# Transposing the attention output on VectorE, and the output product for two tiles at once

## The chip, the cores and the metric

The kernel runs on one core of a Trainium2 chip. The metric is the device time of one execution in microseconds. The program is a single launch; three runs of the kernel before are given, and one more execution was taken with the hardware profiler.

## What is computed

The input is `x` of shape (4, 512, 128): four batches of 512 tokens with 128 features. One causal attention layer with 16 heads of 64 comes first, and then six layers, each with a windowed attention and a feed-forward part. Layer `i`, cut to what matters here:

```python
def local_attention(q, k, v):        # windows of 32 tokens
    bk2, bv2 = look(bk), look(bv)    # keys and values: the window before and the window itself
    sim = einsum('bhwie,bhwje->bhwij', bq, bk2) * 8.0
    attn = softmax(where(mask, -max, sim), -1)
    return einsum('bhwij,bhwje->bhwie', attn, bv2)

def attn_layer(x, Wqkv, qs, ksc, Wo):
    q, k, v = split(x @ Wqkv)        # 16 heads of 64
    q, k = l2norm(q) * qs, l2norm(k) * ksc
    q = q * cos * scale + rotate_half(q) * sin * scale
    k = k * cos * inv + rotate_half(k) * sin * inv
    return local_attention(q, k, v) @ Wo

for i in range(6):
    x = attn_layer(shift_tokens(x), ...) + x
    x = ffn_layer(shift_tokens(x), ...) + x    # layernorm, W1, gelu gate, W2
```

All of it is in float32; the mask is a bfloat16 table.

## The kernel before

**Stages.** The first attention runs for about 560 us and is not touched, apart from its hand-over. Then come the layers. A unit (`class Unit`, line 530) is one tile of 128 tokens of one batch of one layer: 6 layers, 4 batches and 4 tiles `T` give 96 units. `slot(n, ...)` (line 893) is one step of a software pipeline: it makes the scores and the attention of unit `n` (`u`), the output product of unit `n-1` (`prev`), the transposed q and k of unit `n+1` (`nxt`), and the projections of unit `n+2` (`new`). The order of the instructions on each engine is the order in which this function writes them (`tc.manual_schedule`, line 983); the framework adds the waits between engines. Feed-forward steps of an earlier batch are planned into slots (lines 998 to 1008): over four slots these are a token shift and a chunk (T = 0), the mean and a chunk (T = 1), the variance and the second product `out` (T = 2), the scale and a chunk (T = 3). They are `Ffn` (line 757) with `layernorm_steps` (line 92).

**One unit, in the order of the work.** `project` (line 535) makes 128x1024 of q, k or v in a PSUM tile of two banks. `square` (549) is on ACT, `sum_squares` (553) on DVE. `rotate` (558) makes two products on DVE from the same PSUM tile, lines 561 and 567; `add_rotated` (577) adds them on POOL. `inverse_norms` (580) bounds the sums of squares from below on DVE and takes the inverse root: a shift and a subtraction on integers on DVE (84, 85), and three Newton rounds of four small operations on POOL (87 to 90). `over_norm` (585) multiplies on POOL. `transpose_q` and `transpose_k` (654, 659) go through PE and an ACT copy.

`scores` (670) writes the mask with eight matmuls on tiles of 64 rows by 32 columns of the PE array, adds 64 score products, then on DVE takes the maximum `mx` (697) and subtracts it (699). `exponents` (703) is one ACT instruction over 128x1024. `transpose_p` (707) transposes through PE and copies with ACT. `times_v` (712) is PV: window `j` on the rows of the output, the value windows in `u.vw`; two DVE operations per half divide by the denominator (728, 729) into `on`.

`v_windows` (628) copies v to `vt` on ACT, writes that to DRAM and reads it back as overlapping windows with four more DMAs, all on SP's queue. `transpose_o` (736) transposes `on` with eight PE transposes and two ACT copies into `aT`. `project_out_2` (741) is the output product of one tile with eight matmuls of 128 columns, and `residual` (746) adds x on DVE.

**PSUM.** `two_t` (516) hands out three tiles of two banks in rotation, so that scores, PV's first half and v share tile 0 of a slot, q, PV's second half and feed-forward tile 1, and k has tile 2, which is tile 0 of the next slot. `one_t` (520) is a ring of two single banks for transposes and small products.

**Tables of ACT.** Exponentials and Gelu need different tables. After the Gelu of a slot, line 981 runs an exponential on two columns (`prime`), so that the table is there for the next slot.

**Order of a slot before.** PE: scores, q, a feed-forward norm step, output product of `prev`, first half of k and the transposes of p between, second half of k, PV, `qT`, v, `kT`, feed-forward, transposes of `on`. ACT: square of q, exponents, copies of `pT`, square of k, copies of `qT`, `vt`, `kT`, Gelu, copies of `aT`. DVE: `mx`, subtraction, norm step, rotation of q with the residual between, PV's division, sum of q, rotation of k, sum of k, bound, gate.

Of the kernel before, what the change touches and what calls it, by code (L numbers as in the profile page):

```python
# [15 lines left out]
P = 128  # L16
# [16 lines left out]
def body(ctx: ExitStack, tc: tile.TileContext, a, out: bass.AP):  # L33
# [16 lines left out]
    dram = ctx.enter_context(tc.tile_pool(name="dram", bufs=1, space=bass.MemoryType.DRAM))  # L50
# [10 lines left out]
    hsel = const.tile([P, 2], F32, tag="hsel", name="hsel")  # L61
    nc.vector.memset(hsel, 0.0)
    nc.vector.memset(hsel[0:HD, 0:1], 1.0)
    nc.vector.memset(hsel[HD:P, 1:2], 1.0)
# [10 lines left out]
    prime = small.tile([P, 2], F32, tag="prime", name="prime", bufs=1)  # L75


    def rsqrt(v, n, eng):
# [7 lines left out]
        for k in range(3):  # L86
            eng.tensor_tensor(t, y, y, ALU.mult)  # L87
            eng.tensor_tensor(t, t, v, ALU.mult)
            eng.tensor_scalar(t, t, -0.5, 1.5, ALU.mult, ALU.add)
            eng.tensor_tensor(y if k < 2 else v, y, t, ALU.mult)  # L90

    def layernorm_steps(state, bank, inT, outT, g=None, b=None, eng=nc.vector, nt=NT, temp=tmpt, later=None):
# [16 lines left out]
        def var():  # L109
# [5 lines left out]
            then(lambda: rsqrt(rs, nt, eng))  # L115

        def scale():
# [7 lines left out]
            if g is not None:  # L125
                then(lambda: nc.vector.tensor_scalar(h, h, g, b, ALU.mult, ALU.add))
# [363 lines left out]
    s2a = ps2a = s2b = s2 = ps_one = kT_first = vts = vds = None  # L490
# [88 lines left out]

    def inverse_norms(u):  # L580

        nc.vector.tensor_scalar(u.ss, u.ss, 1e-24, None, ALU.max)  # L582
        rsqrt(u.ss, 2 * HEADS, nc.gpsimd)
# [16 lines left out]
    def second_step():  # L600

        nonlocal s2b, ps_one, kT_first, vts, vds
# [5 lines left out]
        vts = [s2b.tile([P, 2, NC, HD + 1], F32, tag=f"vt{j}", name=f"vt{j}") for j in range(2)]  # L608
        for t_ in vts:
            nc.gpsimd.memset(t_[:, :, :, HD : HD + 1], 1.0)  # L610
        vds = [dram.tile([W + S, 2, NC * (HD + 1)], F32, tag=f"vd{j}", name=f"vd{j}") for j in range(2)]
        for d_ in vds:
            nc.sync.dma_start(out=d_[0:W], in_=a["zeros"])
# [14 lines left out]
    def v_windows(u):  # L628


        vt, vd = vts[u.n % 2], vds[u.n // NT % 2]
        src = u.p[2].rearrange("p (c a d) -> p a c d", a=2, d=HD)
        for c in range(2):
            nc.scalar.copy(vt[:, c, :, 0:HD], src[:, c])  # L634
        r0 = u.T * P
        nc.sync.dma_start(out=vd[r0 + W : r0 + W + P], in_=vt.rearrange("p a c d -> p a (c d)"))
        u.vw = s2b.tile([P, NW, NC, HD + 1], F32, tag="vw", name="vw", bufs=2)
        for odd in range(2):
            rows = vd[r0 + odd * W : r0 + odd * W + P].rearrange("(j k) a x -> a k j x", k=2 * W)
            for c in range(2):  # L640
                nc.sync.dma_start(
                    out=u.vw[c * HD : (c + 1) * HD, odd::2].rearrange("p j c d -> p j (c d)"), in_=rows[c]
                )
# [25 lines left out]

    def scores(u):  # L670

        sc = two_t(0, "ps_att")
        for j in range(NW):
            for h in range(2):
                rows = slice(h * HD, (h + 1) * HD)
                mm(  # L676
                    sc[j * W : (j + 1) * W, h, :],
                    lhsT=ident16[rows, h * HD : h * HD + W],
                    rhs=band[rows, min(u.T + j, 1)].unsqueeze(1).to_broadcast([HD, NC, 2 * W]),
                    start=True,  # L680
                    stop=False,
                    skip_group_check=True,
                )
        for c in range(NC):
            for j in range(NW):
                for h in range(2):
                    mm(  # L687
                        sc[j * W : (j + 1) * W, h, c * 2 * W : (c + 1) * 2 * W],
                        lhsT=u.qT[h * HD : (h + 1) * HD, c, j * W : (j + 1) * W],
                        rhs=u.kT[h * HD : (h + 1) * HD, c, j * W : (j + 2) * W],  # L690
                        start=False,
                        stop=True,
                        skip_group_check=True,
                    )
        s3 = sc.rearrange("p a (c n) -> p a c n", n=2 * W)
        mx = small.tile([P, 2, NC], F32, tag="mx", name="mx")
        nc.vector.tensor_reduce(mx, s3, AX.X, ALU.max)
        u.pr = s2.tile([P, NC, 2, 2 * W], F32, tag="pr", name="pr", bufs=2)
        nc.vector.tensor_tensor(
            u.pr.rearrange("p c a n -> p a c n"), s3, mx.unsqueeze(3).to_broadcast([P, 2, NC, 2 * W]), ALU.subtract  # L700
        )

    def exponents(u):
        u.prf = u.pr.rearrange("p c a n -> p (c a n)")
        nc.scalar.activation(u.prf, u.prf, AF.Exp)

    def transpose_p(u, g):
        if g == 0:
            u.pT = s2.tile([P, NC, P], F32, tag="pT", name="pT", bufs=2)
        transposed(u.prf, g, u.pT, 0)  # L710

    def times_v(u, g):
        if g == 0:
            u.on = s2.tile([P, NC, 2, HD], F32, tag="on", name="on", bufs=1)
        o = two_t(g, "ps_att")
        for c in range(4):
            for j in range(NW):
                for h in range(2):
                    mm(  # L719
                        o[j * W : (j + 1) * W, h, c * (HD + 1) : (c + 1) * (HD + 1)],  # L720
                        lhsT=u.pT[h * HD : (h + 1) * HD, 4 * g + c, j * W : (j + 1) * W],
# [451 lines left out]
```

## Time and profile before

| | us |
|---|---|
| median of three runs | 2180.27 (2177.94 to 2182.57) |
| profiled execution | 2177.22 |
| its span | 2175.2 |
| PE busy (matmul) | 2127.0 |
| PE weight loads | 1424.5 |
| DVE busy | 1720.1 |
| ACT busy | 1380.8 |
| POOL busy | 1508.3 |
| first slot's scores, from the start | 561.0 |
| last slot's scores, from the start | 2134.3 |

The busy times count instructions at work on an engine within the span; matmuls are pipelined, so PE's busy time tells that something was in the array, not how well it was filled. The time of an execution is 2.0 us longer than the span of its profile. Most lines below are of three kinds: groups (line of code, engine, operation, output from inputs, shape, count, busy us, mean ns, idle time before and what ended it), timelines (start us, length us, engine, line, operation, count, and in brackets the idle time before), and stages (length, then busy us of PE, PE's weight loads, DVE, ACT and POOL, the granted clock, DMA share and GB/s).

### The profile page before, as it was taken

How to read it: one execution, taken by the hardware profiler on the slowest of the kernel's cores; microseconds unless marked ns; L12 is line 12 of the kernel's file. 1: busy time of each engine (PE TensorE's matmuls, PEld its weight loads, DVE VectorE, ACT ScalarE, POOL GpSimd, SP SyncE). 2: the span in 40 equal slices, each digit the busy share in tenths (PEclk: the TensorE clock that was granted, in tenths of full speed). 3: DMA queues.
4: the chain of work that ended last, by engine and by line, in shares of the span. 5: the costliest groups of instructions: out<-in, count | busy, mean ns of one | idle time of the engine just before them, and what ended most of it. 6: DMA issues, size and time to landing. Idle time of an engine off the chain costs nothing.

```text
span 2175.2 us, 80486 instructions
## 1 busy us (share of the span) xinstructions
PE 2127.0 (98%) x35150; PEld 1424.5 (65%) x35150; DVE 1720.1 (79%) x2501; ACT 1380.8 (63%) x2677; POOL 1508.3 (69%) x2279
## 2 busy tenths in 40 slices
PE   7999999999999999999999999999999999999998
PEld 5655656555566666676667666666766676667665
DVE  3776766767778888888888888888888888888884
ACT  3675656755455667666676666676666666666764
POOL 2554545455787787777877877877877778778773
PEclk8999999999999999999999999999999999999999
DMA  3000000000343353343434334433453344434331
GB/s 126 1 1 1 1 1 1 1 1 1 100 111 99 99 135 101 101 114 99 120 111 109 102 100 128 116 91 111 106 136 92 101 119 112 115 103 114 91 101 41
DMA packets 88812, 180.17 MB, mean 83 GB/s; under 512 B 9327, under 2 KB 23405, under 8 KB 88429
## 3 DMA queue, kind: packets, MB, share of 16 engines
q1 hardware_dynamic: 87756, 173.31, 29.3%
q8 instruction: 278, 4.55, 0.9%
q10 hardware_dynamic: 704, 1.70, 0.2%
q14 instruction: 74, 0.60, 0.1%
HBM read 122.81 MB, written 52.43 MB: 81 GB/s over the span
## 4 chain that ended last, share of the span: by engine, by line
PE 87%; DVE 9%; POOL 1%; ACT 1%; issue 1%; DMA 0%; SPq 0%; DVEq 0%; POOLq 0%; ACTq 0%
PE ps_proj L539 21%; PE ps_one L649 15%; PE ps_one L744 7%; PE ps_att L719 6%; PE ps_sc L299 6%; PE ps_att L687 5%; PE ps_o L384 5%; PE ps_pt L364 5%; PE ps_proj L808 3%; PE ps_proj L788 2%; PE ps_proj L789 2%; PE ps_pj L278 1%; PE ps_att L676 1%; DVE ss L556 1%; PE ps_pj L268 1%; DVE ss L582 1%
## 5 line engine op out<-in xcount | busy, mean ns | idle before, releaser
L578 POOL TENSOR_TENSOR rot<-rot,t 128x1024 f32<-128x1024 f32 x192 | 454.3, 2367 | 176.2 <-DVE t L567 161.4
L539 PE MATMUL ps_proj<-wqkv,xs 128*128 128x512 f32 x1152 | 569.6, 602 | 0.2
L353 POOL TENSOR_TENSOR pr<-pr,den 128x1024 f32<-128x1024 f32 x128 | 240.9, 1892 | 248.9 <-DVE den L350 239.0
L586 POOL TENSOR_TENSOR rot<-rot,ss 128x1024 f32<-128x1024 f32 x192 | 361.8, 1905 | 7.4
L551 ACT ACTIVATE sq<-ps_proj 128x1024 f32<-128x1024 f32 x192 | 196.5, 1024 | 172.4 <-PE ps_proj L539 145.0
L539 PEld LDWEIGHTS ps_proj<-wqkv,xs 128*128 128x128 f32 x1152 | 188.5, 190 | 102.9 <-issue 93.8
L561 DVE TENSOR_TENSOR rot<-ps_proj,lt 128x1024 f32<-128x1024 f32 x192 | 233.8, 1217 | 6.0 <-ACT sq L551 5.2
L567 DVE TENSOR_TENSOR t<-ps_proj,lt 128x1024 f32<-128x1024 f32 x192 | 233.2, 1215 | 0.0
L556 DVE TENSOR_REDUCE ss<-sq 128x16 f32<-128x1024 f32 x192 | 232.3, 1210 | 0.0
L339 ACT ACTIVATE pr<-ps_sc,nm 128x128 f32<-128x128 f32 (+3 forms) x448 | 220.3, 509 | 11.8 <-DVE nm L326 8.6
L649 PEld LDWEIGHTS ps_one<-ident,rot 128*128 128x128 f32 x1536 | 171.6, 141 | 66.9 <-issue 43.3
L649 PE MATMUL ps_one<-ident,rot 128*128 128x128 f32 x1536 | 204.6, 276 | 5.2 <-POOL rot L586 4.5
L326 DVE TENSOR_REDUCE nm<-ps_sc 128x2 f32<-128x1024 f32 x128 | 156.0, 1219 | 64.6 <-PE ps_sc L314 64.5
L744 PEld LDWEIGHTS ps_one<-aT,wo 128*128 128x128 f32 x1536 | 182.9, 192 | 23.7 <-issue 23.0
L652 ACT COPY pT<-ps_one 128x512 f32<-128x512 f32 x192 | 110.1, 586 | 136.5 <-PE ps_one L649 136.4
L744 PE MATMUL ps_one<-aT,wo 128*128 128x128 f32 x1536 | 189.2, 276 | 0.4 <-DVE rs L114 0.3
L719 PEld LDWEIGHTS ps_att<-vw,pT 64*32 64x32 f32 x12288 | 130.9, 105 | 77.0 <-ACT pT L652 69.0
L728 DVE RECIPROCAL rden<-ps_att 128x8 f32<-128x8 f32 x192 | 39.0, 203 | 174.0 <-PE ps_att L719 173.9
L634 ACT COPY vt<-ps_proj 128x512 f32<-128x512 f32 x192 | 103.2, 590 | 97.2 <-PE ps_proj L539 90.9
L652 ACT COPY qT<-ps_one 128x512 f32<-128x512 f32 x192 | 103.1, 589 | 96.0 <-PE ps_one L649 96.0
L87 POOL TENSOR_TENSOR yt<-y 128x32 f32<-128x32 f32 (+2 forms) x384 | 87.7, 228 | 108.0 <-DVE y L85 62.0
L364 PEld LDWEIGHTS ps_pt<-ident,pr 128*128 128x128 f32 x1024 | 117.2, 141 | 58.5 <-issue 47.7
(171 smaller groups left out, 4164.2 us busy)
## 6 DMA issues: line engine op xcount, KB each, us to landing
vw<-vd SPq DMA_DIRECT2D x384, 260.0 KB, 4.9
vd<-vt SPq DMA_DIRECT2D x96, 520.0 KB, 2.7
wqkv<-in_wqkv_dram SPq DMA_DIRECT2D x18, 512.0 KB, 4.9
wo<-in_wo_dram SPq DMA_DIRECT2D x6, 512.0 KB, 7.2
w<-in_w_dram SPq DMA_DIRECT2D x6, 341.0 KB, 6.3
xr<-in_x_dram SPq DMA_DIRECT2D x3, 256.0 KB, 7.4
scales<-in_scales_dram SPq DMA_DIRECT2D x6, 128.0 KB, 4.5
w<-in_w_dram SPq DMA_DIRECT2D x12, 64.0 KB, 5.5
```

The costliest lines, as they stand in the source:

```text
L339: nc.scalar.activation(self.pr[:, h, cols], self.sc[:, h, cols], AF.Exp, bias=self.nm[:, part_, h : h + 1], accum_out=self.den[:, part_, h ...
L353: nc.gpsimd.tensor_tensor(self.pr, self.pr, self.den[:, 0].unsqueeze(2).to_broadcast([P, 2, S]), ALU.mult)
L364: nc.tensor.transpose(pt[:, k * P : (k + 1) * P], self.pr[:, h, k * P : (k + 1) * P], ident)
L539: mm(p[:, c, :], lhsT=u.xs[:, u.T * P : (u.T + 1) * P], rhs=wpart[j][:, c * 512 : (c + 1) * 512], start=True, stop=True,)
L556: nc.vector.tensor_reduce(u.ss[:, j * HEADS : (j + 1) * HEADS], heads(u.sq[j]), AX.X, ALU.add)
L561: nc.vector.tensor_tensor(heads(t0), heads(pf), lt[:, u.T, 2 * j].unsqueeze(1).to_broadcast([P, HEADS, HD]), ALU.mult)
L567: nc.vector.tensor_tensor(t1.rearrange("p (h t d) -> p h t d", t=2, d=half), pf.rearrange("p (h t d) -> p h t d", t=2, d=half)[:, :, ::-1, :],
L578: nc.gpsimd.tensor_tensor(u.r[j], u.r[j], u.t1, ALU.add)
L586: nc.gpsimd.tensor_tensor(heads(u.r[j]), heads(u.r[j]), u.ss[:, j * HEADS : (j + 1) * HEADS].unsqueeze(2).to_broadcast([P, HEADS, HD]), AL ...
L649: nc.tensor.transpose(tp[:, c * P : (c + 1) * P], src[:, (4 * g + c) * P : (4 * g + c + 1) * P], ident)
L719: mm(o[j * W : (j + 1) * W, h, c * (HD + 1) : (c + 1) * (HD + 1)], lhsT=u.pT[h * HD : (h + 1) * HD, 4 * g + c, j * W : (j + 1) * W], rhs=u ...
L744: mm(y[:, 0:P], lhsT=wo_w[0][:, c, :], rhs=u.aT[:, c, :], start=(c == 0), stop=(c == NC - 1))
```

## The change

**Attention output.** PV's output rows become 32 tokens for each of four chunks of heads, instead of four windows of tokens, so that a transpose of 32x32 blocks brings features onto the partitions. `transpose_o` becomes one DVE `transpose` of 128x1024; PE's eight transposes and ACT's two copies go. The rows of `wo` are put in the matching order before the launch. `project_out_2` and `residual` take two tiles at a time, in the slots with T = 0 and T = 2.

**V.** The value windows are no longer read back from DRAM. Odd windows read `vt` itself (now three buffers), even windows a copy `vs` that is shifted by 32 tokens with two DMAs from SBUF to SBUF, issued after PV of the slot before. Scores write to other places (`PLACES`), so that the probabilities lie on the partitions of their keys after the transpose.

**Exponents.** DVE subtracts the maximum for four of eight chunks; for the other four ACT makes eight exponents of 128x64 from PSUM, with the negated maximum as bias. The square of q stands after the exponents.

**Inverse norms.** The bound moves to POOL. The inverse root becomes Ln and Exp on ACT and one Newton round on POOL, and it stands at the end of the slot it belongs to (it was put off to the next slot where no Gelu ran). The feed-forward norm gets the same root; its scaling by g and b moves from DVE to ACT. The small exponential `prime` becomes an explicit table load.

**Order.** The k projection is whole, ahead of the transposes of p; PV stands between the two products of k's rotation on DVE. `new` is the unit `n+2` as before.

```diff
     def inverse_norms(u):
-        nc.vector.tensor_scalar(u.ss, u.ss, 1e-24, None, ALU.max)
-        rsqrt(u.ss, 2 * HEADS, nc.gpsimd)
+        v, eng = u.ss, nc.gpsimd
+        nc.scalar.activation(y, v, AF.Ln, scale=float(1 << 16))
+        nc.scalar.activation(y, y, AF.Exp, scale=-0.5)
+        eng.tensor_tensor(t, y, y, ALU.mult)
+        eng.tensor_tensor(t, t, v, ALU.mult)
+        eng.tensor_scalar(t, t, -0.5 * (1 << 24), 1.5 * (1 << 8), ALU.mult, ALU.add)
+        eng.tensor_tensor(v, y, t, ALU.mult)
...
+    def keep_v(u):
         src = u.p[2].rearrange("p (c a d) -> p a c d", a=2, d=HD)
         for c in range(2):
+            nc.scalar.copy(vts[u.n % 3][:, c, :, 0:HD], src[:, c])
+    def shift_v(u):
+        u.vs = s2b.tile([P, 2, NC, HD + 1], F32, tag="vs", name="vs")
+        nc.sync.dma_start(out=u.vs[W:P], in_=vts[u.n % 3][0 : P - W])
+        nc.sync.dma_start(out=u.vs[0:W], in_=vts[(u.n - 1) % 3][P - W : P] if u.T else a["zeros"])
...
+    PLACES = [(j, h, j // 2, (h ^ j // 2) * HD + j % 2 * W) for j in range(NW) for h in range(2)]
...
-        nc.vector.tensor_reduce(mx, s3, AX.X, ALU.max)
+        nc.vector.tensor_reduce(u.mx, s3, AX.X, ALU.max, negate=True)
         nc.vector.tensor_tensor(
-            u.pr.rearrange("p c a n -> p a c n"), s3, mx.unsqueeze(3).to_broadcast([P, 2, NC, 2 * W]), ALU.subtract
+            u.pr[:, 0:4].rearrange("p c a n -> p a c n"),
+            s3[:, :, 0:4],
+            u.mx[:, :, 0:4].unsqueeze(3).to_broadcast([P, 2, 4, 2 * W]),
+            ALU.add,
         )
     def exponents(u):
-        nc.scalar.activation(u.prf, u.prf, AF.Exp)
+        for c in range(4, NC):
+            for x_ in range(2):
+                nc.scalar.activation(
+                    u.pr[:, c, x_],
+                    u.sc[:, x_, c * 2 * W : (c + 1) * 2 * W],
+                    AF.Exp,
+                    bias=u.mx[:, x_, c : c + 1],
+                )
+        nc.scalar.activation(u.prf[:, 0:512], u.prf[:, 0:512], AF.Exp)
...
     def transpose_o(u):
-        u.aT = s2.tile([P, NC, P], F32, tag="aT", name="aT", bufs=2)
-        for g in range(2):
-            transposed(u.on.rearrange("p c a d -> p (c a d)"), g, u.aT, 0)
+        nc.vector.transpose(
+            out=u.aT[:, u.T % 2].rearrange("p g n -> p (g n)"), in_=u.on.rearrange("p g a c d -> p (g a c d)")
+        )
-    def project_out_2(u):
-            mm(y[:, 0:P], lhsT=wo_w[0][:, c, :], rhs=u.aT[:, c, :], start=(c == 0), stop=(c == NC - 1))
+    def project_out_2(us):
+            mm(
+                y[:, 0 : n * P],
+                lhsT=wo_w[0][:, k, :],
+                rhs=us[0].aT[:, t0 : t0 + n, g].rearrange("p t (j f) -> p t j f", f=P)[:, :, :, f0 : f0 + W],
+                start=(k == 0),
+                stop=(k == NC - 1),
+            )
...
     def slot(n, norm, move, geglu):
+        pair = [unit(n - 2), prev] if prev and prev.T % 2 else None
         if new:
             do_project(new, 0)
-            square(new, 0)
         if u:
             exponents(u)
-        while behind:
-            behind.pop(0)()
+        if new:
+            square(new, 0)
+        def steps_between():
+            for f in norm:
+                f()
+            if pair:
+                project_out_2(pair)
+        if new:
+            rotate(new, 0, [steps_between])
             add_rotated(new, 0)
+        if pair:
+            residual(pair)
         for f in move:
             f()
+        if new:
+            do_project(new, 1)
+        if u:
+            transpose_p(u, 1)
             transpose_p(u, 0)
         if new:
             square(new, 1)
+        def attend():
+            if u:
+                times_v(u, 1)
+                times_v(u, 0)
+                transpose_o(u)
+            if nxt:
+                shift_v(nxt)
+        if new:
+            rotate(new, 1, [attend])
+            add_rotated(new, 1)
         while later:
             later.pop(0)()
         if new:
             sum_squares(new, 0)
-            rotate(new, 1)
-            add_rotated(new, 1)
             sum_squares(new, 1)
         if nxt:
             transpose_q(nxt)
         if new:
+            do_project(new, 2)
+            keep_v(new)
         if nxt:
             transpose_k(nxt)
             carry_k(nxt, follower(nxt))
         if new:
+            guard(new)
         for f in geglu:
             f()
-        if u:
-            transpose_o(u)
         if geglu and unit(n + 1):
-            nc.scalar.activation(prime, hsel, AF.Exp)
+            nc.scalar.preload_act_table_set("natural_log_exp_and_others")
+        if new:
+            inverse_norms(new)
+            over_norm(new, 0)
+            over_norm(new, 1)
```

## The prediction

> **What bounds the kernel now.** I read the page's busy shares and chain of waits first, then busy time by stage, then one slot after another in the timelines of PE and DVE, then the groups for prices. A slot is one pass of `slot`; four slots (a slot's tile is T = 3, 0, 1, 2 in the rows below) take one batch of four tiles with its feed-forward part.
>
> ```profile
> PE 2127.0 (98%) x35150; PEld 1424.5 (65%) x35150; DVE 1720.1 (79%) x2501; ACT 1380.8 (63%) x2677; POOL 1508.3 (69%) x2279
> PE 87%; DVE 9%; POOL 1%; ACT 1%; issue 1%; DMA 0%; SPq 0%; DVEq 0%; POOLq 0%; ACTq 0%
> ```
> ```profile
> 1207.13:1224.53 17.40, 17.40 (x445) 12.55 (x445) 14.68 (x20) 10.63 (x18) 11.43 (x17) 1.00 0.48 125
> 1224.53:1240.72 16.19, 16.19 (x377) 11.22 (x360) 14.52 (x18) 12.19 (x19) 14.42 (x24) 1.00 0.37 102
> 1240.72:1256.42 15.70, 15.46 (x232) 10.12 (x230) 13.76 (x19) 11.10 (x16) 11.27 (x18) 1.00 0.38 104
> 1256.42:1273.38 16.96, 16.96 (x329) 11.96 (x309) 14.25 (x21) 10.14 (x17) 14.24 (x30) 1.00 0.36 97
> ```
>
> The stages (length, then PE, weight loads, DVE, ACT, POOL busy, clock, DMA) show PE without a hole at clock 1.00 and DVE at 14.3 of 16.6 us. Over slots 12 to 87 the mean slot is 16.61 us, four are 66.5. The timeline of PE confirms that each group starts when the one before has issued:
>
> ```profile
> 1223.31 0.41 PE L676 MATMUL ps_att<-band,ident 64*32 64x512 bf16 x8
> 1226.75 1.95 PE L744 MATMUL ps_one<-aT,wo 128*128 128x128 f32 x16
> 1228.53 1.02 PE L539 MATMUL ps_proj<-wqkv,xs 128*128 128x512 f32 x2
> 1238.05 1.04 PE L649 MATMUL ps_one<-ident,on 128*128 128x128 f32 x8
> 1239.02 0.41 PE L676 MATMUL ps_att<-band,ident 64*32 64x512 bf16 x8
> ```
>
> Start to start, the transposes of `on` cost 0.97 us, the output product 1.78. Taken likewise from that view: band and scores 1.70, q or k projection 1.82 whole, `pT` 0.88, PV 1.45, `qT` 0.93, v projection 1.72, `kT` 0.87, a feed-forward chunk 1.72, `out` 2.58, mean 0.86, var 0.81, scale 0.44.
>
> ```profile
> 1225.86 1.21 DVE L697 TENSOR_REDUCE mx<-ps_att 128x16 f32<-128x1024 f32 x1
> 1227.11 1.23 DVE L699 TENSOR_TENSOR pr<-ps_att,mx 128x1024 f32<-128x1024 f32 x1
> 1228.25 1.22 DVE L561 TENSOR_TENSOR rot<-ps_proj,lt 128x1024 f32<-128x1024 f32 x1
> 1232.26 0.21 DVE L728 RECIPROCAL rden<-ps_att 128x8 f32<-128x8 f32 x1 [1.47 <-PE ps_att L719]
> 1232.51 0.69 DVE L729 TENSOR_TENSOR on<-ps_att,rden 128x512 f32<-128x512 f32 x1
> 1238.58 2.25 DVE L582 TENSOR_SCALAR ss<-ss 128x32 f32<-128x32 f32 x1
> ```
> ```profile
> DVE rot L561 <- ACT sq L551: 5.2, 20, 1.0
> ```
> ```profile
> L339 ACT ACTIVATE pr<-ps_sc,nm 128x128 f32<-128x128 f32 x128 | 46.3, 375 | 7.7 <-DVE nm L326 7.7
> L652 ACT COPY aT<-ps_one 128x512 f32<-128x512 f32 x192 | 102.5, 588 | 38.8 <-PE ps_one L649 38.8
> ```
>
> The waits hold the fact that decides: the first rotation product does not start before the square of the same PSUM tile has ended on ACT. In none of the 192 pairs does it; in 39 it starts 0.03 us after. Both only read, but the program orders them. Now ACT squares *before* the exponents, so this costs 5.2 us in all.
>
> **The change, part by part.**
>
> PE, four slots: the transposes of `on` go, 4 x 0.97 = 3.9. The output product made for two tiles saves little: an instruction takes 0.111 us for 128 columns and 0.43 for 512, so 16 of 256 columns take 16 x 0.215 + 0.06 = 3.5 against 2 x 1.8 to 1.99. Summing the pieces above: 61.6 against 66.5. Were PE still the bound, this is -4.9 us in four slots.
>
> Removed elsewhere: ACT's two `aT` copies (1.07), DVE's maximum L582 (1.36 mean, for 32 columns) and two bit operations (0.46), eight of POOL's twelve small steps; POOL takes the maximum (about 0.25). The five DMAs per unit through DRAM become two from SBUF to SBUF; the earlier ones landed in 2.7 and 4.9 us, and the new pair, issued after PV, has the more than 10 us until the next PV. POOL's queue (maximum behind `carry_k`, then ACT's Ln and Exp, four steps, two 1.9 us products) ends some 8 us into the next slot, before `qT` and `kT` need them. Covered; free.
>
> Added to DVE: a 128x1024 transpose, which no row shows. Bounds: 0.61 (start to start of a 512-column operation) to 2.3 (two passes of 1.13); I take 1.2, as every 1024-column operation. The Trainium skill, "VectorE: DVE Perf Modes", section "The three transpose paths", gives 311 ns for 128x128 bf16; eight such would be an estimated 2.5 us, and the total below would be some 58 us more. No run here shows it yet.
>
> Added to ACT: eight exponents of 128x64 from PSUM with a bias. By L339's 375 ns at 128 columns and the 0.84 ns per column between 512 (624) and 1024 (1052), one takes 0.32; back to back ACT overlaps 0.105, so 0.215 each (bounds 0.155 and 0.32). They wait for DVE's half subtraction too: the order of after shows the 512-column exponent with no wait of its own, so the first of the eight carries it.
>
> Scores move to other places, and the two row tiles now share a bank. No row has that; bounds 0 to another 1.70 (the tiles in turn); nearest is the present 1.47 for 128 matmuls, so I take 0; the far end, +163 us in 96 slots, stays outside the range. The Trainium skill, "TensorEngine Tiling (Array Packing)", "Gotcha 1: PSUM Pressure", says that row tiles cannot use one PSUM bank at once; that would add up to 1.70 a slot, 163 us.
>
> **The path, by hand.** Let M be the start of mx. Sub starts at M+1.25, ends +1.94. Exponents of 64: +1.98 to +3.82; of 512: to +4.34. The square of q is now *behind* them: +4.24 to +5.26. So DVE, idle 3.3 us, starts rotation at +5.30; the norm's operation in odd slots (0.68) at +6.43; second product +7.03 to +8.24. PV's second half writes that PSUM tile, so it waits: +8.35 to +9.1 (before, PV's wait was hidden). Then PE: `qT`, v, `kT`, chunk: 0.93 + 1.72 + 0.87 + 1.72, next scores at M+14.3. DVE goes on: k's first product to +9.29, two reciprocals and products to 11.1, transpose 12.3, k's second product, two sums, gate: next mx at M+16.3, as PE allows (14.3 + 1.95). So an odd slot, mx to the next scores, is 14.3.
>
> Even slot, from its scores: q 3.52, output product 7.02, k 8.84. `pT` starts there; copies on ACT from +0.69, 0.47 apart; the square of k, now behind them, 10.47 to 11.49; k's first product 11.52 (it too waits for the square, and stands ahead of PV's reciprocals); reciprocals and products to 14.43; transpose 14.46; k's second 15.58; sums 16.71, 17.84; gate 18.97; mx 19.63. PE is ready for mx at 17.0 + 1.95 = 18.95, so DVE ends last. With var and `out` (T=2) PE ends last: 18.66 + 1.95 = 20.61.
>
> Four slots: 19.63 + 14.34 + 20.61 + 14.34 = 68.9, +2.4 us. 22 groups: +54. The eight slots without feed-forward, by the same chain: 31.9 a pair against 30.6, +5. Head and tail: 0 (the tail swaps 0.97 of PE and a copy for 1.2 on DVE, and gains 0.8 of exponents). Total +59 on the execution's 2177.2 (span 2175.2 and 2.0 around it): 2236; the median of the runs lies 3 above, so **2239**. Bounds: exponents -23 to +40 (8 x the difference in the two odd slots of each group), transpose -13 (only T=0 gains) to +49: 2203 to 2328.
>
> **The rivals.**
>
> *PE stays the bound: faster.* If squares do not hold the rotations up, 61.6 us remain plus the wait of PV for the first `pT` copy, 0.5 a slot (1.4 from first transpose to PV, 0.9 of it filled by the second transposes): 63.6, -2.9 x 24 = -69, 2111. For: PE is the bound today, DVE's busy sum falls. Against: the 0.03 us in 39 pairs. It decides if rotation starts before the square ends, or if exponents cost nearly nothing.
>
> *DVE's transpose is held up by POOL: slower still.* L582 takes 1.3 to 2.3 us for 32 columns beside POOL's 2.37 us addition. If the transpose, SBUF to SBUF too, waits so, 1.1 more at T=0 and 2, +49: 2288. Against: by the chain POOL is idle at that moment. It decides from 0.7 us of delay (T=0 at once, T=2 after 0.2).
>
> *It balances:* exponents at 0.155 and a transpose under 1 bring +20 to +30; with some overlap I missed, nothing. About 2180.
>
> **Numbers.** Forecast 0.65, PE-bound 0.19, transpose held 0.11, balance 0.05. Forecast's own range 2203 to 2328; that both of its costs sit at their upper ends is unlikely, so above I stop at 2300. Downwards I reach into the faster rival: 2115. Chances with 0.2% (4.4 us) as what a measurement tells from none: faster 0.21, same 0.04, slower 0.75.
>
> **What would show it.** Right: PE's busy share falls to about 94% or below, with holes ahead of PV in odd slots released by DVE's second rotation product, and DVE rotations waiting on ACT squares for some 3 us a slot, 250 us or more in all. The transposes near 1.2 us, exponents near 0.32. Wrong: no such waits, slots under 16.6 us, odd ones about 14.5 from scores to scores; or score matmuls over 1.7 us a slot.

## The result, and the profile after

The changed kernel takes 2333.72 us (median of 4 runs, 2331.55 to 2340.45), the kernel before 2179.43 beside it (2177.94 to 2182.57): a ratio of 1.0711, 95% interval 1.0685 to 1.0738. That is slower, as forecast, but 154 us slower, not 59, and above the top of the range. The span is 2333.9 us against 2175.2: the layers (first slot's scores to last slot's) took 164.3 us more, the head 1.1 and the tail 4.4 less.

The page of the changed kernel, busy shares and chain of waits:

```profile
PE 2097.3 (90%) x33630; PEld 1338.2 (57%) x33630; DVE 1592.6 (68%) x2193; ACT 1466.5 (63%) x3446; POOL 1318.2 (56%) x1432
PE 64%; DVE 17%; ACT 15%; issue 3%; DMA 0%; POOL 0%; SPq 0%; ACTq 0%
```

PE does less work (30 us) and is idle 237 us of the span where it was idle 48. The chain that was PE's to 87% now has 32% on DVE and ACT, although each is busy for about two thirds of the time: they take turns.

The stages of one group of four slots, T = 3, 0, 1, 2 (length, then busy us of PE, weight loads, DVE, ACT, POOL, granted clock, DMA share, GB/s):

```profile
1272.19:1288.72 16.53, 13.99 (x309) 8.76 (x309) 12.12 (x15) 9.87 (x24) 9.57 (x14) 1.00 0.17 46
1288.72:1307.53 18.81, 16.90 (x321) 11.39 (x320) 12.70 (x16) 12.11 (x25) 12.65 (x17) 1.00 0.11 30
1307.53:1324.59 17.06, 14.41 (x307) 8.64 (x306) 12.87 (x16) 12.52 (x26) 10.10 (x11) 1.00 0.12 34
1324.59:1345.15 20.56, 18.65 (x331) 12.66 (x330) 13.62 (x17) 13.26 (x27) 10.98 (x11) 1.00 0.10 27
```

Every slot has 1.9 to 2.7 us in which PE does nothing; before, three of four had none. Mean lengths over slots 12 to 87, T = 0, 1, 2, 3: before 15.86, 16.85, 17.50, 16.25, together 66.5; after 18.81, 17.60, 20.55, 16.85, together 73.8. So +7.35 us in four slots, where +2.4 was forecast.

The waits of the changed kernel (engine, tile and line, released by; us in all, times, longest):

```profile
POOL rot L587 <- DVE t L576: 488.1, 163, 6.6
DVE rot L570 <- ACT sq L560: 424.6, 143, 3.6
...
PEld ps_one L661 <- ACT pT L664: 112.2, 91, 1.7
...
PE ps_one L661 <- ACT pT L664: 90.7, 91, 1.4
...
PE ps_att L750 <- DVE t L576: 52.6, 46, 1.2
PE ps_proj L548 <- DVE rden L759: 50.9, 43, 1.2
```

The second line is the one the prediction rested on: 5.2 us before, 424.6 now. The last four are PE's (PEld is its weight loads), and two kinds of them were not in its sum: the transposes of p (661) wait for a copy of p, and the v projection (548) waits for PV's division.

An even slot in the timeline of the changed kernel (T = 0; its scores start at 1288.72 and its maximum at 1290.99):

```profile
1295.12 1.07 ACT L560 ACTIVATE sq<-ps_proj 128x1024 f32<-128x1024 f32 x1
1296.23 1.23 DVE L570 TENSOR_TENSOR rot<-ps_proj,lt 128x1024 f32<-128x1024 f32 x1 [3.30 <-ACT sq L560]
...
1297.33 0.60 PE L661 MATMUL ps_one<-ident,pr 128*128 128x128 f32 x4
...
1297.96 0.59 ACT L664 COPY pT<-ps_one 128x512 f32<-128x512 f32 x1 [1.77 <-PE ps_one L661]
...
1298.50 0.41 DVE L799 TENSOR_TENSOR xT<-ps_one,xT 128x256 f32<-128x256 f32 x1
...
1298.60 0.66 PE L661 MATMUL ps_one<-ident,pr 128*128 128x128 f32 x4 [0.68 <-ACT pT L664]
...
1299.30 0.58 ACT L664 COPY pT<-ps_one 128x512 f32<-128x512 f32 x1 [0.74 <-PE ps_one L661]
...
1299.78 1.03 ACT L560 ACTIVATE sq<-ps_proj 128x1024 f32<-128x1024 f32 x1
...
1300.84 1.23 DVE L570 TENSOR_TENSOR rot<-ps_proj,lt 128x1024 f32<-128x1024 f32 x1 [1.92 <-ACT sq L560]
...
1301.98 0.20 DVE L759 RECIPROCAL rden<-ps_att 128x8 f32<-128x8 f32 x1
...
1303.06 1.95 PE L548 MATMUL ps_proj<-wqkv,xs 128*128 128x512 f32 x4 [1.23 <-DVE rden L759]
...
1303.78 1.25 DVE L769 STREAM_TRANSPOSE aT<-on 128x1024 f32<-128x1024 f32 x1
```

Read it as one chain. The square of q, behind the exponents, ends at 1296.19; 0.04 us later the rotation of q starts, DVE having been idle for 3.30. Behind the rotation on DVE stands the residual (799), which empties one of the two single banks of `one_t`. While that bank is held, the eight transposes of p must share the other: the residual ends at 1298.91, but the second four start at 1298.60, 0.05 us after the first copy has ended, so it is the first four's bank that they take. So the second copy is 1.34 us behind the first, the square of k stands behind that, the rotation of k behind the square, PV's division behind the rotation, and PE's v projection, which takes the PSUM tile that PV's first half leaves, behind the division. So far this is a reading of one timeline; the experiments test its links.

An odd slot (T = 3; maximum at 1273.91):

```profile
1279.17 1.23 DVE L570 TENSOR_TENSOR rot<-ps_proj,lt 128x1024 f32<-128x1024 f32 x1 [3.30 <-ACT sq L560]
...
1279.67 0.66 PE L661 MATMUL ps_one<-ident,pr 128*128 128x128 f32 x4 [1.28 <-ACT pT L664]
...
1280.91 1.22 DVE L576 TENSOR_TENSOR t<-ps_proj,lt 128x1024 f32<-128x1024 f32 x1
...
1282.27 0.46 PE L750 MATMUL ps_att<-vs,pT 64*32 64x65 f32 x31 [1.16 <-DVE t L576]
```

Here PE waits twice: for the copy of p, and for the second rotation product, whose PSUM tile PV's second half takes.

Groups of the changed kernel for the operations that no row showed before:

```profile
L769 DVE STREAM_TRANSPOSE aT<-on 128x1024 f32<-128x1024 f32 x96 | 119.6, 1245 | 3.3
L725 ACT ACTIVATE pr<-ps_att,mx 128x64 f32<-128x64 f32 x768 | 167.6, 329 | 100.6 <-DVE pr L712 99.6 <-DVE rs L120 0.9
```

The transpose takes 1.245 us and stands waiting for nothing; eight small exponents take 1.74 us in one go in the timeline, 0.20 apart.

### The profile page after: what moved, and what is told of

Its sections match the earlier page's. It is cut to its first block, busy times and chain, and to the rows that moved or that the text cites. A ratio compares the mean times of both kernels' runs of the same rounds, so it can differ in the third digit from the quotient of the medians.

```text
span 2333.9 us, 76662 instructions
## 1 busy us (share of the span) xinstructions
PE 2097.3 (90%) x33630; PEld 1338.2 (57%) x33630; DVE 1592.6 (68%) x2193; ACT 1466.5 (63%) x3446; POOL 1318.2 (56%) x1432
## 4 chain that ended last, share of the span: by engine, by line
PE 64%; DVE 17%; ACT 15%; issue 3%; DMA 0%; POOL 0%; SPq 0%; ACTq 0%
PE ps_proj L548 15%; PE ps_one L781 7%; PE ps_one L661 6%; PE ps_sc L308 5%; PE ps_o L393 5%; PE ps_pt L373 4%; PE ps_att L700 4%; DVE rot L570 4%; ACT pr L725 4%; ACT sq L560 4%; PE ps_proj L855 3%; DVE t L576 2%; DVE mx L710 2%; DVE on L760 2%; ACT pT L664 2%
## 5 line engine op out<-in xcount | busy, mean ns | idle before, releaser
L570 DVE TENSOR_TENSOR rot<-ps_proj,lt 128x1024 f32<-128x1024 f32 x192 | 234.7, 1222 | 427.8 <-ACT sq L560 424.6
L548 PEld LDWEIGHTS ps_proj<-wqkv,xs 128*128 128x128 f32 x1152 | 204.9, 193 | 244.6 <-issue 223.1
L725 ACT ACTIVATE pr<-ps_att,mx 128x64 f32<-128x64 f32 x768 | 167.6, 329 | 100.6 <-DVE pr L712 99.6
L565 DVE TENSOR_REDUCE ss<-sq 128x16 f32<-128x1024 f32 x192 | 223.3, 1203 | 0.0
L661 PEld LDWEIGHTS ps_one<-ident,rot 128*128 128x128 f32 x1536 | 182.1, 147 | 63.7 <-issue 56.2
L661 PE MATMUL ps_one<-ident,rot 128*128 128x128 f32 x1536 | 216.4, 286 | 0.5 <-ACT qT L664 0.3
L661 PE MATMUL ps_one<-ident,pr 128*128 128x128 f32 x768 | 121.6, 281 | 96.5 <-ACT pT L664 90.7
L560 ACT ACTIVATE sq<-ps_proj 128x1024 f32<-128x1024 f32 x192 | 201.7, 1051 | 5.5 <-PE ps_proj L548 5.5
L661 PEld LDWEIGHTS ps_one<-ident,pr 128*128 128x128 f32 x768 | 88.6, 141 | 169.2 <-ACT pT L664 112.2
L781 PE MATMUL ps_one<-aT,wo 128*128 128x256 f32 (+1 forms) x784 | 175.9, 377 | 0.3 <-ACT tmp_t L875 0.2
L781 PEld LDWEIGHTS ps_one<-aT,wo 128*128 128x128 f32 x784 | 144.8, 190 | 29.1 <-issue 11.5
```

Of the source, the lines that this page charges most:

```text
L548: mm(p[:, c, :], lhsT=u.xs[:, u.T * P : (u.T + 1) * P], rhs=wpart[j][:, c * 512 : (c + 1) * 512], start=True, stop=True,)
L560: nc.scalar.activation(u.sq[j], u.p[j], AF.Square)
L565: nc.vector.tensor_reduce(u.ss[:, j * HEADS : (j + 1) * HEADS], heads(u.sq[j]), AX.X, ALU.add)
L570: nc.vector.tensor_tensor(heads(t0), heads(pf), lt[:, u.T, 2 * j].unsqueeze(1).to_broadcast([P, HEADS, HD]), ALU.mult)
L661: nc.tensor.transpose(tp[:, c * P : (c + 1) * P], src[:, (4 * g + c) * P : (4 * g + c + 1) * P], ident)
L725: nc.scalar.activation(u.pr[:, c, x_], u.sc[:, x_, c * 2 * W : (c + 1) * 2 * W], AF.Exp, bias=u.mx[:, x_, c : c + 1],)
```

## The experiments

All ratios are against the kernel before, measured beside each, with the 95% interval. Slots are means over slots 12 to 87 in the order T = 0, 1, 2, 3; in the changed kernel they are 18.81, 17.60, 20.55, 16.85. Except for the last, each edit stands in the changed kernel.

**The two squares, alone and together.** If ACT's order is the cause, moving a square forward gives back the wait behind it. The square of q goes back to where it stood; the square of k goes ahead of the copies of p, where it did not stand before the change either.

```diff
 q_square_first
-        if u:
-            exponents(u)
         if new:
             square(new, 0)
+        if u:
+            exponents(u)
 k_square_first
             do_project(new, 1)
+            square(new, 1)
         if u:
             transpose_p(u, 1)
             transpose_p(u, 0)
-        if new:
-            square(new, 1)
```

> The changed kernel with one order turned: the square of q ahead of the exponents on ACT, as it was before the change. Theory A (DVE's rotations wait for squares queued behind other ACT work, and what stands behind the rotations on DVE then holds PE): the first rotation product starts some 2.7 us earlier in each slot, the bank that the norm step or the residual reads comes free in time, the second half of the transposes of p no longer waits for the first copy; odd slots about 1.4 us and even slots about 0.7 us shorter, in all about -100 us: 2230 (2200 to 2260). Theory B (DVE's new transpose and the other work moved onto DVE and ACT are the cost, order matters little): within 20 us of 2334. Theory C (Ln and Exp of the inverse norms hold ACT ahead of the exponents): no gain or a loss, 2330 to 2370, because the exponents start still later.

> The changed kernel with the square of k ahead of the two copies of the transposed p on ACT. Theory A: in even slots k's first rotation product starts some 2 us earlier, PV's first half is divided earlier, so the v projection waits less; the copies themselves come about 0.6 us later; even slots about 1 us shorter, odd slots the same: about -48 us, 2286 (2260 to 2310). Theory B: within 20 us of 2334. Theory C: unchanged, 2334.

> The changed kernel with both squares ahead: q's before the exponents, k's before the copies of p. Theory A: even slots about 1.4 us, odd slots about 1.5 us shorter, together about -140 us: 2194 (2160 to 2230), about level with the kernel before. Theory B: within 30 us of 2334. Theory C: 2320 or more.

The square of q first: 2235.27, 1.0246 [1.0231, 1.0262], slots 17.97, 15.80, 19.75, 15.80. The square of k first: 2296.63, 1.0527 [1.0511, 1.0542], slots 17.80, 17.66, 18.87, 17.43. Both, which is both edits together: 2169.31, 0.9942 [0.9925, 0.9958], slots 17.12, 15.10, 18.91, 15.28. The first two came within 11 us of what the theory of ACT's order gave; the third is 25 us better. Theory B (order matters little) and theory C (Ln and Exp hold ACT ahead of the exponents) have fallen: neither allows 98 us or 164. Two instructions moved in ACT's queue, with no work saved anywhere, are worth 164 us, more than the whole loss. The effects are not a sum (98 + 37 = 135). One reason can be read from the records: with the square of k first alone, TensorE ran at half clock (see the end) for 119.5 us of the layers, against 64.9 in the changed kernel and none with both. That one late square also keeps the other's wait on the chain is my reading, not shown by itself.

**PV's division ahead of the rotation of k.** This takes away the second new wait and leaves both squares late.

```diff
+        attend()
         if new:
-            rotate(new, 1, [attend])
+            rotate(new, 1)
             add_rotated(new, 1)
-        else:
-            attend()
```

> The changed kernel with PV's division and the DVE transpose ahead of both of k's rotation products, so that PV's division does not stand behind a product that waits for the square of k. Theory A as I hold it now (the wait of the v projection for PV's division counts in even slots, and what is gained there is lost where k's rotation, the sums and the gate come later): between -30 and +20 us, 2304 to 2354. If the wait for PV's division alone were the whole loss: about -70 us, 2265. Theory B: unchanged.

2254.74, 1.0329 [1.0314, 1.0345], slots 17.34, 16.73, 19.10, 16.83. The expectation missed: I had taken this order as nearly indifferent, and the measured time lies near the other sum, 2265. PE in an even slot of this run:

```profile
1297.45 1.09 PE L661 MATMUL ps_one<-ident,rot 128*128 128x128 f32 x8
1298.38 1.88 PE L548 MATMUL ps_proj<-wqkv,xs 128*128 128x512 f32 x4
```

The v projection follows `qT` at once; in the changed kernel 1.23 us lay between. Even slots are 1.46 us shorter, 64 us in 44 of them. The T = 1 slots are 0.87 us shorter, and 0.54 of that is the half clock, which none of them has in this run. So the change's own move of PV into the middle of k's rotation costs some 79 us as long as the square of k is late, about 64 of them by the wait of v.

**The norm step and the residual ahead of the rotation of q.** If the bank that they hold is what parts the transposes of p, reading it first should join them.

```diff
-        if new:
-            rotate(new, 0, [steps_between])
-            add_rotated(new, 0)
-        else:
-            steps_between()
+        steps_between()
         if pair:
             residual(pair)
+        if new:
+            rotate(new, 0)
+            add_rotated(new, 0)
```

> The changed kernel with the feed-forward norm step, the output product and the residual ahead of q's rotation on DVE, so that DVE frees their single PSUM bank while it would wait for the square of q. Theory A1 (the second half of the transposes of p waits for the first copy because the other single bank is still to be read on DVE): that wait goes, the copies and the square of k come 0.4 to 0.8 us earlier in every slot, odd slots 0.6 us more by the norm step moved into idle time: about -65 us, 2268 (2240 to 2295). Theory A2 (only the squares count, the bank is a by-product): within 15 us of 2334.

2261.12, 1.0365 [1.0350, 1.0381], slots 17.97, 16.88, 19.71, 15.96. Met. PE in an even slot:

```profile
1300.01 1.04 PE L661 MATMUL ps_one<-ident,pr 128*128 128x128 f32 x8
1301.29 0.46 PE L750 MATMUL ps_att<-vs,pT 64*32 64x65 f32 x32 [0.24 <-ACT pT L664]
...
1304.89 1.95 PE L548 MATMUL ps_proj<-wqkv,xs 128*128 128x512 f32 x4 [1.07 <-DVE rden L759]
```

The eight transposes stand in one piece, and PV follows 1.28 us after their start instead of 1.86; the wait of v is still there. The whole is 73 us, but not all of it is the bank. In even slots, 0.84 us shorter, the residual's new place changes nothing else that PE waits for: 37 us, and the held bank is shown as the first new wait. In odd slots the edit also takes the norm step out from between the two products of q's rotation, for the second of which PV waits; at full clock, maximum to next scores falls from 14.80 to 14.22 us, the 0.6 expected of that, and the rest of their 35 us is clock.

**Both of these together.**

> The changed kernel with both edits that took a wait away by themselves: norm step, output product and residual ahead of q's rotation (2261 alone), and PV's division ahead of k's rotation (2255 alone), both squares still late. If the two waits are two places of loss that add: -73 and -79 from 2334, 2182 (2165 to 2195). If they are one chain in which the later wait swallows the earlier: 2225 or more.

2209.29, 1.0126 [1.0109, 1.0142], slots 16.67, 17.55, 18.41, 15.63: between the two expectations, 124 us gained of the 152 if the two added. In even slots they nearly add: 2.14 us each, against 1.47 + 0.84 (T = 0) and 1.45 + 0.84 (T = 2). What is missing fits the clock. In the records of this run TensorE is at half clock for 3.41 us in every T = 1 slot of slots 12 to 87 and in no other of them; from the maximum to the next scores T = 1 slots take 15.28 us and T = 3 slots 13.91, which differ by 0.02 us in the changed kernel at full clock, and 1.37 x 22 = 30 is about the 28 that is missing.

**The transpose on DVE, doubled and undone.** Is it an error of the change to have put the transpose on DVE?

```diff
 transpose_twice
-        nc.vector.transpose(...)
+        for _ in range(2):
+            nc.vector.transpose(...)
 transpose_on_pe
-        nc.vector.transpose(...)
+        for g in range(2):
+            transposed(u.on.rearrange("p g a c d -> p (g a c d)"), g, ..., 0)
...
         for f in behind:
             f()
+        if u:
+            transpose_o(u)
```

In the second, the transposes of `on` are again eight PE transposes and two ACT copies at the end of the slot, with `wo` in its first order; the output product stays for two tiles.

> The changed kernel with the DVE transpose of each tile made twice, 1.25 us more on DVE in every slot. Theory A: DVE has slack there, since the gate waits 0.8 us for the Gelu and mx waits for the scores in one slot of four: about 0.7 us in four slots, +17 us, 2350 (2335 to 2370). Theory B (DVE is the bound, its transpose costs what it takes): 96 times 1.17, +112 us, 2445.

> The changed kernel with the attention output transposed by eight PE transposes and two ACT copies at the end of the slot, as before the change, and the weights in their old order; the output product still for two tiles. Theory A (the DVE transpose is a gain, the loss lies in the order): PE gets 0.97 us more per slot, of which some is hidden by waits: +50 to +95 us, 2385 to 2430. Theory B (the DVE transpose is what made it slower): down by 60 us or more, below 2275.

On PE: 2437.33, 1.1176 [1.1159, 1.1194], 104 us slower than the changed kernel, 7 above the top of what theory A gave. DVE's transpose by itself is a gain, and the rival that makes it the culprit has fallen. Done twice: 2400.76, 1.1009 [1.0978, 1.1039], slots 18.81, 18.75, 20.55, 18.06; neither theory has it. From the scores to the next maximum, the part in which the transpose lies, even slots grow by 0.44 (T = 0) and 0.13 (T = 2): some 13 us, about what was expected of the path. Most of the rest of the 67 lies in odd slots between the maximum and the next scores, a stretch whose path does not pass the transpose: 0.71 us (T = 1) and 1.08 (T = 3), 39 us in 22 groups; the remainder lies in slots at the beginning and the end. At its shortest the stretch is 14.8 us as in the changed kernel, in the 3 of 38 odd slots that have full clock; on the mean it is 16.0 (T = 1) and 16.2 (T = 3). The stage of one at half clock, of the run with two transposes:

```profile
1219.05:1236.79 17.74, 15.20 (x309) 9.95 (x308) 14.27 (x18) 9.96 (x24) 10.68 (x14) 0.90 0.12 33
```

The granted clock is 0.90: the run has 194.6 us at half clock in the layers, the changed kernel 64.9. More on that at the end.

**One exponent instead of nine.** DVE subtracts the maximum for all eight chunks and ACT makes one 128x1024 exponent, as before the change.

```diff
-            u.pr[:, 0:4].rearrange("p c a n -> p a c n"), s3[:, :, 0:4], ...
+            u.pr.rearrange("p c a n -> p a c n"), s3, ...
...
-        for c in range(4, NC):
-            for x_ in range(2): ...
-        nc.scalar.activation(u.prf[:, 0:512], u.prf[:, 0:512], AF.Exp)
+        nc.scalar.activation(u.prf, u.prf, AF.Exp)
```

> The changed kernel with the exponents as before the change: DVE subtracts for all eight chunks and ACT makes one exponent of 128x1024. Theory A: the square of q ends about 0.75 us earlier, which odd slots get in full and even slots in part: -35 to -60 us, 2275 to 2300. If eight short exponents save more on DVE than they cost in ACT's queue: 2334 or more.

2275.93, 1.0438 [1.0413, 1.0463], slots 18.64, 16.67, 19.82, 15.86. Met: what stands in front of the squares costs 58 us. The split takes 0.54 us of subtraction from DVE in each slot, 52 in all, and DVE waits 110 us longer for squares by it (424.6 against 314.6).

**The old order around the new layout.** Square of q first, k in two halves with the transposes of p between, square of k, PV's division, rotation of k: these as before, with everything else of the change (the norm step and the residual keep their new places on DVE). And the same with one exponent.

```diff
+            square(new, 0)
         if u:
             exponents(u)
...
-            do_project(new, 1)
+            do_project(new, 1, 0, 1)
         if u:
             transpose_p(u, 1)
             transpose_p(u, 0)
         if new:
+            do_project(new, 1, 1)
             square(new, 1)
...
+        attend()
         if new:
-            rotate(new, 1, [attend])
+            rotate(new, 1)
```

> The changed kernel with the order of the kernel before around it: square of q ahead of the exponents, the k projection in two halves with the transposes of p between them, the square of k after the second half, PV's division ahead of k's rotation. Kept: the DVE transpose, the output product for two tiles, V shifted in SBUF, Ln and Exp, eight short exponents. Theory A (only order lost the time; the layout itself takes about 4.9 us per four slots from PE): no wait of PE for the copies of p is left, PE is nearly full again, 62.5 to 63.5 us in four slots: 2095 (2075 to 2130). Theory B (DVE and ACT now bound the slot, both squares first is about the best): 2150 to 2175.

> The kernel with the old order and the new layout (2142), with the exponents as before the change as well. In odd slots PE waits 1.3 us for the exponents between the transposes of p; one exponent of 1.05 us in place of 1.74 and 0.5 after a subtraction 0.54 longer brings them 0.6 us forward: -0.6 us in two of four slots, 2113 (2100 to 2130). If DVE is the bound there: 2142 or more.

The first: 2142.35, 0.9826 [0.9811, 0.9840], slots 16.33, 15.10, 18.22, 15.19; between the two expectations. The second: 2127.15, 0.9753 [0.9736, 0.9769], slots 16.52, 14.80, 18.60, 14.82, the fastest of all: 2.5% below the kernel before and 8.9% below the changed one (2127.15 / 2333.72). What kept the first from the 2095 that PE's work would allow is in its waits:

```profile
PEld ps_one L661 <- ACT pr L725: 80.7, 195, 1.5
DVE rot L570 <- ACT sq L560: 67.5, 96, 3.5
```

The transposes of p now wait for the nine exponents; the waits for squares are down to 67.5 us. The busy shares of the second:

```profile
PE 2039.6 (96%) x33630; PEld 1297.9 (61%) x33630; DVE 1650.1 (78%) x2193; ACT 1365.5 (64%) x2678; POOL 1316.0 (62%) x1432
```

So what is left of the change (the layout, the transpose, the two-tile product, V in SBUF and the new inverse norms) brings some 54 us together; the order and the split exponent took back 207.

**The same move in the kernel before.** Only the square of q goes behind the exponents, in the old kernel.

```diff
             do_project(new, 0)
-            square(new, 0)
         if u:
             exponents(u)
+        if new:
+            square(new, 0)
```

> The kernel before with one order turned: the square of q behind the exponents on ACT. Theory A as the traces show it: DVE's first rotation starts some 2 us later, but PV stands well behind it and DVE had 1.3 us of idle time before PV's division, so little is lost: +0 to +30 us, 2181 to 2211. If the order of the square alone is worth what it is worth in the changed kernel: +100 us, 2280.

2197.34, 1.0078 [1.0063, 1.0093]: +16 us, as expected of the theory. Its rotations wait 149.6 us for squares (5.2 before), yet the time grows by only a tenth of that. As I read it, a late rotation hurts by what stands behind it, and there one exponent was in front, the square of k was in its old place and the division ahead of k's rotation.

## Why the prediction failed in size

**What held.** The mechanism is the one named: rotations wait for squares behind exponents, 424.6 us (said: 250 or more), PE's share 90% (said: 94% or below), holes ahead of PV in odd slots released by DVE's second product. The prices were right: transpose 1.245 (taken 1.2, where the estimate from the Trainium skill, "VectorE: DVE Perf Modes", "The three transpose paths", is 2.5), exponent 0.329 (0.32), wo pair 3.45 (3.5). The 128 score matmuls, now with two row tiles in one bank, took 1.39 us in every slot, where before it was 1.39 at the shortest and 1.5 on the mean; the far end of +1.70, which the Trainium skill, "TensorEngine Tiling (Array Packing)", "Gotcha 1: PSUM Pressure", speaks for, does not show here. V's windows cost no wait: no DMA is in the chain. The rivals were wrong: PE is not the bound, and the transpose is not held by POOL.

**What failed.** By the same two stretches as in the prediction, M being the start of a maximum:

| us | forecast | measured | difference |
|---|---|---|---|
| odd, M to next scores, at full clock | 14.34 | 14.79 | +0.45, twice |
| odd, mean over T = 1 and T = 3 | 14.34 | 15.33, 15.12 | +0.54, +0.33 more |
| T = 0, scores to next M | 19.63 | 21.08 | +1.45 |
| T = 2, scores to next M | 20.61 | 22.28 | +1.67 |
| four slots | 68.9 | 73.8 | +4.9 |

In the table, "odd" stands for T = 1 and T = 3. Over 22 groups 4.9 us is 108; the eight slots without feed-forward, the head and the tail came out some 8 below what was taken, which leaves the 100 us between 2236 and the profiled execution.

1. *"copies on ACT from +0.69, 0.47 apart."* They are 1.34 apart. I let both halves of `pT` go to PE at once because `one_t` has two banks, and did not ask who held the other one: the norm step or the residual, which DVE reads late because it stands behind the rotation that I had just found late. The square of k came at +11.06 instead of 10.47, k's first product at +12.12 instead of 11.52, and the transpose at +15.06 instead of 14.46: 0.60 us, carried to the end of the slot. Run norm_before_rotation shows it.

2. *PE "ready at 17.0", with v following `qT`.* I followed the chain from the rotation of k to the division to the transpose on DVE, but let PE go on as if v needed nothing from it. v takes the PSUM tile of PV's first half, as the description of PSUM ahead of the prediction has it, so it waits for the division: 1.23 us. At T = 2 this is PE's own path: v starts 15.23 us after the scores, where the pieces give 13.49. At T = 0 the copies of v and kT, the table load and the Gelu come later on ACT, and the gate (line 843 on DVE, the product with Gelu's result) waits 0.75 us for the Gelu before the next slot's maximum at 1309.80; with the 0.60 and 0.1 of small gaps that is the 1.45. Run pv_before_k_rotation shows it. The gate at T = 0 and v at T = 2 in the changed kernel:

```profile
1309.13 0.75 DVE L843 SCALAR_TENSOR_TENSOR tmp_t<-ps_proj,vecs,tmp_t 128x512 f32<-128x512 f32 x1 [0.75 <-ACT tmp_t L839]
...
1339.82 1.96 PE L548 MATMUL ps_proj<-wqkv,xs 128*128 128x512 f32 x4 [1.23 <-DVE rden L759]
```

3. *The odd slot.* It held to 0.05 us up to PV's second half (M + 8.36, said 8.35); behind it small gaps between `qT`, v and the band add 0.45. Two readings of the kernel before were slightly off and change nothing here: the transposes of p take 0.93 start to start in the T = 0 slot, not 0.88, and PE has 0.24 us without work in the third of the four stages.

4. *The clock.* Pieces taken from the timeline of before hold at full clock only. In 11 of the 38 odd slots from 12 to 87, PE ran at half clock for one or two times 3.41 us; from the maximum to the next scores these took 15.61 to 17.37 us, the other 27 took 14.79 to 14.95. Together that is (0.54 + 0.33) x 22 = 19 us. That this is the clock is read from the records and from where the time lies; no run changes the clock alone.

The step that failed is one and the same in 1 and 2: I priced the late squares on the chain that I followed, and put at nothing what is queued behind the late rotations. In even slots that came to 1.45 and 1.67 us, 3.1 of the 4.9 in four slots; the clock is 0.87 more and the small gaps of odd slots 0.9. A rotation on DVE that is late leaves its own tile, a bank of `one_t`, and PV's tile late, and each has its own customer on PE.

Not tried by themselves: the shift of V in SBUF, Ln and Exp in the inverse norms, the output product for two tiles, the explicit table load (ACT's loads at line 1024 are 88 where there were 66).

## What to carry to other kernels

Where two engines read one PSUM tile and the program orders them, the place of the reading instruction in the queue of an engine with time to spare can be a place on the path: on ACT, busy 63% of the time, two squares behind the exponents and the copies of p instead of ahead of them cost 164 us. When a move makes one instruction late, list every tile, bank and queue that it holds, and follow each to its customer, not only along the chain in hand. A change that loses may still hold a gain: undo its order separately from its layout before it is dropped (here 2127 against 2179 and 2334 us).

## What was not expected of the hardware

**Half the clock behind short holes.** The stages of the changed kernel around one odd slot, cut on the grid of 3.41 us on which the clock changes:

```profile
938.24:941.65 3.41, 3.41 (x11) 1.57 (x10) 1.29 (x2) 2.44 (x11) 2.52 (x5) 1.00 0.00 0
941.65:945.06 3.41, 1.76 (x71) 1.19 (x69) 2.19 (x3) 2.66 (x5) 2.20 (x2) 1.00 0.00 0
945.06:948.47 3.41, 2.50 (x71) 2.37 (x72) 3.34 (x6) 1.26 (x3) 2.36 (x1) 0.50 0.21 54
948.47:951.89 3.42, 3.42 (x7) 1.60 (x6) 3.38 (x4) 0.93 (x2) 0.73 (x1) 0.50 0.36 112
951.89:955.30 3.41, 3.41 (x54) 1.82 (x54) 1.38 (x2) 3.00 (x5) 2.31 (x3) 1.00 0.00 0
```

In the second stretch PE is busy 1.76 of 3.41 us (52%); in the next two it gets half the clock. The work done there shows it too, in the timeline of PE:

```profile
948.84 3.40 PE L548 MATMUL ps_proj<-wqkv,xs 128*128 128x512 f32 x4
```

The same four matmuls take 1.95 in the even slot shown above. In the layers of the changed kernel the clock fell 14 times, each time after a stretch with PE busy 32 to 52%, and these are the 14 lowest of all; stretches at 53% and above were not followed by half clock there. This is no sharp rule: with the square of k first alone a stretch at 42% was not followed by it, and with the old order around the new layout three at 67 to 68% were. The Trainium skill, "TensorE: Matmul & The Clock Gate", "What's actually happening", gives the same half rate and the same length of a window, but puts the fall after an idle window; here a window half full was enough, its longest hole 1.40 us. In all, half clock took 3.4 us of the layers in the kernel before, 64.9 in the changed one, 194.6 with the transpose done twice, and none with both squares first. A hole on PE can cost more than its length: behind this one of 1.40 us, the stretch from the maximum to the next scores took 17.14 us, 2.35 more than the 14.79 of such slots at full clock.

**Reads of one PSUM tile.** No rotation product starts before the square of the same tile has ended, in any run. The Trainium skill, "PSUM — Partial Sum Buffer", "PSUM bank collisions raise a hardware error", gives the ground: two engines may not access the same bank within the same partitions at the same time, reads included. No run here lets the two reads overlap. So by that page the wait can't be dropped, only moved, which is what the first runs did.
